# Where the attention's values are summed: two units behind, across sequences, out of one ring of three buffers

## The chip, the core and the metric

One core of a Trainium2 chip runs the whole program. The metric is the device time of one execution in microseconds. The engines are TensorE (PE; its weight loads are listed as PEld), VectorE (DVE), ScalarE (ACT), GpSimd (POOL) and SyncE (SP), whose queue issues most DMAs here. [...]

## The reference

The input is 4 sequences of 1024 tokens with 256 features. Four residual layers follow each other, each behind a layer norm: a linear recurrence with a small MLP, a sparse feed-forward layer (two gated branches that keep the top 32 of 256 features), an attention, and the same feed-forward layer again. The change is in the attention:

```python
q = (x @ Wq.T).reshape(b, t, N_HEADS, HEAD_DIM)
kv_latent = x @ Wkv_down.T
k = (kv_latent @ Wk_up.T).reshape(b, t, N_HEADS, HEAD_DIM)
v = (kv_latent @ Wv_up.T).reshape(b, t, N_HEADS, HEAD_DIM)
scores = jnp.einsum('bqhd,bkhd->bhqk', q, k) * scale
attn = jax.nn.softmax(scores, axis=-1)
out = jnp.einsum('bhqk,bkhd->bqhd', attn, v)
return out.reshape(b, t, N_HEADS * HEAD_DIM) @ Wo.T
```

There are 8 heads of 64 columns, keys and values come from one latent of 64 columns, and the softmax runs over all 1024 tokens.

## The kernel before

The weights are folded, so that the queries meet the latent itself, and the values that are summed are the latent too. Products that need accuracy are made of a high and a low part: `kh` and `kl` for the keys, `la` in f32 or two f16 parts `lb` for the values.

**Units.** `heads` (line 856) goes through one sequence in 32 units. A unit is 128 queries (`q`) of one pair of heads (`g`), and it has two halves (`j`), one head each. There are two blocks of 512 queries (`nb`), so 4 sequences make 128 units and 256 halves. A half does this: four score products into the PSUM tile `sc` (line 886, two buffers), the negated maximum over 1024 keys (line 890, DVE), the exponential with its sum into `ssum` (line 894, ACT) into `pr` (three buffers). Then the probabilities must be transposed, since the product with the values sums over keys.

**Two ways to transpose.** In units with even `q` the probabilities are cast to f16 (line 897, ACT), the remainder is taken on POOL (line 898), and both go through a transposing DMA from SP's queue (line 899) into the tiles `d0` and `d1`, of which there are two each. In units with odd `q` PE transposes in f32 (line 905) into the PSUM tiles `t` (two buffers), and ACT, in the last sequence DVE for one half, copies them (lines 908 and 910) into `p0` and `p1`, of which there is one each.

**The sums.** `values_sum` (line 920) takes the reciprocal of the row sums (DVE), spreads it over 64 columns (line 926, POOL, tile `rows`), multiplies values and transposed probabilities (line 930: 16 products for an f32 unit, 48 for an f16 unit), transposes the reciprocals (line 938), copies them (line 940) and multiplies (line 941) into `on`. Its PSUM bank has the tag `s`, which has two buffers and is shared with all the side work. Two lists hold the units whose sums are due. A unit of the `pending` list (f32) is summed in the first half of the next f16 unit, a unit of the `late` list (f16) in the second half of the next f16 unit. At the end of each sequence what is left in both lists is summed at once (lines 917 and 918). The last group of the last sequence has its units in the order 0, 2, 1, 3.

**Side work.** `merge` (line 963) interleaves the halves of `heads` with the rest by written step numbers: the queries of the next pair, the next sequence's keys and values, the output products (`output`, line 943), the feed-forward tiles of the layer before (24 of 32 tiles run here), and the heads of the next feed-forward layer. That is program order. A planner then decides the final order of each engine's queue from its own estimate of when operands and buffers are free, so a sum may stand several halves behind its place in the program.

## Time and profile before

| | |
|---|---|
| median of 3 runs | 1529.46 us (1526.32 to 1533.48) |
| the profiled execution | 1528.76 us, span 1527.0 us |
| attention stage, first score product to last product of the attention | 376 to 1303 us |
| score products, line 886 | 346.3 us of PE in 1024 matmuls |
| sums, line 930, f32 and f16 | 144.0 and 103.4 us of PE |
| transposes on PE, line 905 | 138.3 us |
| maxima, line 890 | 308.5 us of DVE |
| exponentials, line 894 | 285.9 us of ACT |
| remainders, line 898 | 273.5 us of POOL |
| transposing DMAs, line 899 | 128, 512 KB each read in f16, median 1.92 us on SP's queue |

A line of a group gives the source line, engine, operation, tiles (written <- read), shape and count, then busy time and the mean of one in ns, then the idle time of that engine just before these instructions and which instruction ended it. Busy times of one engine overlap a little where matmuls are pipelined. A wait names the waiting tile and line and the instruction that ended the wait. Granted clock is the share of TensorE's full clock that it was given.

### The profile page before, as it was taken

The page shows a single profiled execution, that of the slowest core. Times are in us where ns is not written, and L with a number is a line of the kernel's source. Part 1 is how long each engine was busy: PE and PEld are TensorE (multiplying, and loading weights), DVE is VectorE, ACT ScalarE, POOL GpSimd, SP SyncE. Part 2 cuts the span into 40 slices and gives each one's busy share as a digit, 9 for nine tenths or more (in the row PEclk, how much of TensorE's full clock was granted, in tenths as well). Part 3 has the DMA queues.
Part 4 walks back from the last instruction along what each step waited for, and adds up shares of the span by engine and source line. Part 5 has one row for each costly group of instructions (what it writes and reads, how often), then busy time and mean ns, then how long its engine had stood idle before and what let it go on. Part 6 is the DMA issues. An engine that isn't in the chain of part 4 may idle for free. (4 is left out here: it accounts for less than half of the span.)

```text
span 1527.0 us, 28727 instructions
## 1 busy us (share of the span) xinstructions
PE 1286.5 (84%) x10134; PEld 955.6 (63%) x10136; DVE 1184.6 (78%) x3682; ACT 1017.5 (67%) x2152; POOL 680.3 (45%) x849
## 2 busy tenths in 40 slices
PE   4879998697898898888998989889999999566675
PEld 3535465376677766766776767677777777334454
DVE  8976665697868887878768687777676675599998
ACT  5353433566887877797777787877777776475674
POOL 2033332161545454544544554454344444067776
PEclk9999999698999999999999999999999999688899
DMA  3110000321454343434433445334344545000000
GB/s 118 32 41 15 21 21 21 128 97 49 84 93 90 61 77 73 77 70 82 82 74 60 72 79 86 61 61 83 68 82 79 92 86 96 1 15 24 22 25 28
DMA packets 288609, 96.51 MB, mean 63 GB/s; under 512 B 268233, under 2 KB 284626, under 8 KB 288466
## 3 DMA queue, kind: packets, MB, share of 16 engines
q1 hardware_dynamic: 283024, 88.50, 28.7%
q10 hardware_dynamic: 5442, 6.18, 1.2%
q8 instruction: 80, 1.31, 0.4%
q14 instruction: 63, 0.52, 0.1%
HBM read 16.01 MB, written 11.53 MB: 18 GB/s over the span
## 5 line engine op out<-in xcount | busy, mean ns | idle before, releaser
L898 POOL TENSOR_TENSOR pd<-pr,pd 128x1024 f16<-128x1024 f32 x128 | 273.5, 2141 | 247.6 <-ACT pd L897 185.7
L890 DVE TENSOR_REDUCE nm<-sc 128x1 f32<-128x1024 f32 x256 | 308.5, 1217 | 78.9 <-PE sc L886 77.5
L894 ACT ACTIVATE pr<-sc,nm 128x1024 f32<-128x1024 f32 x256 | 285.9, 1119 | 84.6 <-DVE nm L892 47.0
L886 PE MATMUL sc<-kh,qs 128*128 128x512 f32 x512 | 184.3, 438 | 26.4 <-ACT pr L894 18.8
L886 PE MATMUL sc<-kl,qs 128*128 128x512 f32 x512 | 162.0, 397 | 0.0
L674 DVE MATCH_REPLACE8 wk<-m,wk 128x256 f32<-128x256 f32 x384 | 154.9, 406 | 0.1
L910 ACT COPY p<-ptp 128x512 f32<-128x512 f32 x224 | 124.1, 590 | 45.3 <-PE ptp L905 33.7
L674 DVE MAX8 m<-wk 128x8 f32<-128x256 f32 x384 | 151.3, 412 | 0.4
L930 PE MATMUL pmo<-p,la 128*64 128x128 f32 x2048 | 144.0, 289 | 6.1 <-ACT ft L524 2.9
L905 PE MATMUL ptp<-ident,pr 128*128 128x128 f32 x1024 | 138.3, 275 | 12.9 <-ACT pr L894 12.4
L930 PEld LDWEIGHTS pmo<-p,la 128*64 128x64 f32 x2048 | 122.8, 144 | 25.0 <-ACT ft L524 5.1
L905 PEld LDWEIGHTS ptp<-ident,pr 128*128 128x128 f32 x1024 | 115.6, 140 | 34.8 <-ACT pr L894 22.2
L897 ACT CAST pd<-pr 128x1024 f16<-128x1024 f32 x128 | 133.5, 1054 | 5.6 <-DMA d<-pd 4.6
L886 PEld LDWEIGHTS sc<-kh,qs 128*128 128x128 f32 x512 | 85.2, 195 | 51.1 <-ACT pr L894 29.8
L886 PEld LDWEIGHTS sc<-kl,qs 128*128 128x128 f32 x512 | 97.0, 190 | 23.2 <-issue 1.4
L930 PE MATMUL pmo<-d,lb 128*64 128x128 f16 x3072 | 103.4, 222 | 7.6 <-DVE qs L853 2.6
L930 PEld LDWEIGHTS <-lb 128*64 128x64 f16 x3072 | 92.2, 111 | 26.3 <-issue 20.1
L628 POOL TENSOR_TENSOR ex<-ex,wk 128x512 f32<-128x512 f32 x61 | 77.6, 1273 | 57.4 <-DVE wk L674 45.5
L926 POOL COPY rows<-rs 128x128 f32<-128x128 f32 x128 | 36.1, 294 | 124.4 <-PE pmo L938 76.3
L941 DVE TENSOR_TENSOR on<-pmo,rb 128x128 f32<-128x128 f32 x128 | 36.4, 285 | 66.8 <-ACT rb L940 66.3
L147 PE MATMUL pt<-ident,xn 128*128 128x128 f32 x256 | 47.8, 309 | 44.5 <-ACT xn L145 32.9
L699 PE MATMUL pf<-wf,vt 128*128 128x256 f32 x288 | 81.2, 427 | 4.6 <-ACT vt L697 4.2
(307 smaller groups left out, 2768.6 us busy)
## 6 DMA issues: line engine op xcount, KB each, us to landing
tt<-ft SPq DMA_DIRECT2D x16, 256.0 KB
tt<-tt SPq DMA_DIRECT2D x8, 512.0 KB
out<-x SPq DMA_DIRECT2D x32, 128.0 KB
x<-in_x ACTq DMA_DIRECT2D x6, 512.0 KB
pf<-pfs SPq DMA_DIRECT2D x12, 256.0 KB
full<-pf SPq DMA_DIRECT2D x24, 128.0 KB
d<-pd SPq DMA_TRANSPOSE x128
wa<-in_w_attn SPq DMA_DIRECT2D x2, 640.0 KB
```

The costliest lines, as they stand in the source:

```text
L147: nc.tensor.transpose(pt[:, k, i * P : (i + 1) * P], xn[:, k * P : (k + 1) * P], ident)
L628: pool.tensor_tensor(ex, ex, wk, ALU.subtract)
L674: ins = make(*args).ins
L699: nc.tensor.matmul(dst, vt[:, k, :], w.wf[:, k, :], start=(k == 0 and bias is None), stop=(k == KD - 1))
L886: nc.tensor.matmul(sc[:, sl], qs[:, j, q * P : (q + 1) * P], kk[:, sl], start=(i == 0), stop=(i == 1))
L890: nc.vector.tensor_reduce(nm, sc, AX.X, ALU.max, negate=True)
L894: nc.scalar.activation(pr, sc, AF.Exp, bias=nm, accum_out=ssum[:, j : j + 1])
L897: nc.scalar.copy(pd[:, 0, :], pr)
L898: nc.gpsimd.tensor_tensor(pd[:, 1, :], pr, pd[:, 0, :], ALU.subtract)
L905: nc.tensor.transpose(pt[:, kk, :], pr[:, kc * P : (kc + 1) * P], self.ident)
L910: nc.scalar.copy(dst, pt)
L930: nc.tensor.matmul(po[j * HD : (j + 1) * HD, 0, :], v, pts[j][:, c, :], start=(n == 0), stop=(n == len(terms) - 1),)
```

## The change

Both lists become one, `due`, which lives in the attention object and so across sequences. Every unit takes one unit out of it: with more than one unit due, the oldest unit's reciprocals are issued in the first half (the new method `reciprocals`) and its sum in the second half. A unit is thus summed in the second half of the second next unit, whatever its kind. Nothing is summed at the end of a sequence, except for the last one, where two units are left. The tiles `d0`, `d1` go; f16 units use `p0` and `p1` too, seen as f16 with twice the columns, and these have three buffers each. `ssum` has six buffers instead of four.

```diff
-        late, pending = [], []
...
-            ssum = sp.tile([P, 2], F32, tag="ssum", name="ssum", bufs=4)
+            ssum = sp.tile([P, 2], F32, tag="ssum", name="ssum", bufs=6)
+            pts = [wp.tile([P, TPB, P], F32, tag=f"p{j}", name=f"p{j}", bufs=3) for j in range(2)]
             if by_dma:
-                pts = [wp.tile([P, 2 * TPB, P], F16, tag=f"d{j}", name=f"d{j}", bufs=2) for j in range(2)]
+                pts = [t.bitcast(F16).rearrange("p c (i q) -> p (c i) q", i=2) for t in pts]
...
             else:
-                pts = [wp.tile([P, TPB, P], F32, tag=f"p{j}", name=f"p{j}") for j in range(2)]
...
-                if j == 0 and pending:
-                    self.values_sum(*pending.pop(0), psum)
-                if j == 1 and late and by_dma != (q > 0 and (b, nb, g) == (B - 1, 1, PAIRS - 1)):
-                    self.values_sum(*late.pop(0), psum)
+                if j == 0 and len(self.due) > 1:
+                    rows = self.reciprocals(self.due[0][2])
+                if j == 1 and len(self.due) > 1:
+                    self.values_sum(*self.due.pop(0), rows, psum)
                 yield
-            (late if by_dma else pending).append((pts, terms, ssum, self.on[b, nb, q][:, g, :]))
-        for args in late + pending:
-            self.values_sum(*args, psum)
+            self.due.append((pts, terms, ssum, self.on[b, nb, q][:, g, :]))
+        if b == B - 1:
+            for unit in self.due:
+                self.values_sum(*unit, self.reciprocals(unit[2]), psum)
...
-    def values_sum(self, pts, terms, ssum, on, psum):
+    def reciprocals(self, ssum):
 
         nc, sp = self.nc, self.sp
         rs = sp.tile([P, 2], F32, tag="rs", name="rs")
         nc.vector.reciprocal(rs, ssum)
         rows = sp.tile([P, 2, HD], F32, tag="rows", name="rows")
         nc.gpsimd.tensor_copy(rows, rs[:, :, None].to_broadcast([P, 2, HD]))
+        return rows
+
+    def values_sum(self, pts, terms, ssum, on, rows, psum):
```

More of the change, by code (lines that the diff above doesn't have):

```diff
@@ L777, in __init__ @@
         self.hp = None
+        self.due = []
         self.k, self.xnt, self.qs, self.on = {}, {}, {}, {}
@@ L926, in values_sum @@
         nc.gpsimd.tensor_copy(rows, rs[:, :, None].to_broadcast([P, 2, HD]))
+        return rows
+    def values_sum(self, pts, terms, ssum, on, rows, psum):
+        nc, sp = self.nc, self.sp
         po = psum.tile([P, 2, P], "s", "pmo")
```

## The prediction

> **What bounds the kernel now.** I read the page first, then the busy time stage by stage, then TensorE's (PE's) own waits in the stage that the diff touches, then who holds a buffer.

> ```profile
> span 1527.0 us, 28727 instructions
> ...
> PE 1286.5 (84%) x10134; PEld 955.6 (63%) x10136; DVE 1184.6 (78%) x3682; ACT 1017.5 (67%) x2152; POOL 680.3 (45%) x849
> ...
> PEclk9999999698999999999999999999999999688899
> ```

> The reader is to see that no engine is saturated over the whole span, and that the clock dips only before and after the middle part. By stage (cut where the score products of line 886 begin and the attention's last product ends, with cuts between at the sequences):

> ```profile
> core 0: us, PE busy (x) PEld busy (x) DVE busy (x) ACT busy (x) POOL busy (x), PEclk, DMA share, GB/s
> 376.00:606.00 230.00, 205.04 (x1996) 160.96 (x1997) 182.25 (x475) 180.43 (x363) 113.28 (x118) 0.99 0.44 80
> 606.00:853.00 247.00, 218.79 (x2143) 173.94 (x2142) 188.62 (x497) 187.78 (x374) 115.47 (x119) 0.97 0.39 74
> 853.00:1096.00 243.00, 215.76 (x2139) 172.06 (x2137) 182.19 (x471) 185.84 (x367) 111.13 (x111) 0.97 0.40 73
> 1096.00:1303.00 207.00, 193.80 (x2125) 157.63 (x2123) 138.93 (x283) 151.60 (x273) 90.17 (x77) 1.00 0.45 83
> 1303.00:1527.00 224.00, 146.23 (x539) 94.94 (x538) 204.02 (x865) 133.64 (x408) 135.95 (x216) 0.84 0.06 20
> ```

> The change lives in the first four rows, 927 us. There PE is busy 205.0 + 218.8 + 215.8 + 193.8 = 833.4 us, so it idles 93.6 us. This stage is paced by PE with small stalls, and 93.6 us is all that any reordering can win. The last row is VectorE's (DVE's) top-k, which the change doesn't touch. What PE's stalls in the stage are:

> ```profile
> PE sc L886 <- ACT pr L894: 18.8, 22, 2.8
> PE ptp L905 <- ACT pr L894: 12.4, 16, 1.8
> PE pt L147 <- DVE qs L853: 9.0, 5, 2.1
> PE sc L886 <- DVE qs L853: 6.7, 7, 1.7
> ...
> L930 PE MATMUL pmo<-p,la 128*64 128x128 f32 x2048 | 144.0, 289 | 6.1 <-ACT ft L524 2.9 <-DVE qs L853 1.8 <-ACT p L910 0.7
> L905 PE MATMUL ptp<-ident,pr 128*128 128x128 f32 x1024 | 138.3, 275 | 12.9 <-ACT pr L894 12.4 <-ACT p L910 0.5
> L930 PE MATMUL pmo<-d,lb 128*64 128x128 f16 x3072 | 103.4, 222 | 7.6 <-DVE qs L853 2.6 <-DMA d<-pd 1.9 <-ACT ex L615 1.9
> ```

> (columns of the first four: total, times, longest.) PE mostly waits for an exponential, to free a score bank or to have something to transpose. The sums of line 930 hardly ever wait for their own data: 0.7 us for a copy by ScalarE (ACT), 1.9 us for a DMA. And the buffers of transposed data, from the lists of line 910 and of SyncE's (SP's) waits:

> ```profile
>   PE ptp L905: 33.7, 32
>   PE pmo L930: 9.0, 4
> ```

> ```profile
> SPq L899 <- POOL pd L898: 238.8, 44, 11.4
> SPq L899 <- PE pmo L930: 194.8, 40, 14.6
> ```

> ACT waited 9.0 us in four places, and SP 194.8 us, until an old sum gave its buffer back. Both rings are already short; SP's wait costs nothing as long as the sum stands far enough back in PE's queue.

> **The change part by part.** A unit is 128 queries of two heads; a half is one head of it. Costs per item from steady stretches of the timeline: four score products 1.6 us, eight transposes 1.1 us, an f32 sum 2.0 us, an f16 sum 1.5 us, its transposed reciprocals 0.33 us.

> *Work.* No product, exponential, copy or DMA comes or goes: 64 f32 and 64 f16 sums, 128 reciprocals, 128 DMA transposes in both. The SBUF is the same: 2x2 and 2x1 tiles of 4 KB a partition before, 2x3 now. So 833 us of PE work stays; only the 93.6 us move.

> *No flush between sequences.* At 856.12 and 857.83 us the two flushed sums of a sequence start without idle time in front of them; their 3.8 us of work is only moved. The gaps around the three boundaries (821 to 860, 577 to 609, 1069 to 1085 us: 6.0, 5.3 and 3.2 us of PE idle) end on exponentials, layer norms and the query split, which all stay. Between 0 and -14.5 us; near the row of the sums themselves, which is 0: I take **-2 us**.

> *Reciprocals half a unit earlier.* PE's transposes of them (line 938) have no idle time before them now, so PE gains 0. On GpSimd (POOL) the copy of 0.29 us waits 76.3 us in all for line 938 two sums earlier, and the subtractions of line 898, whose result the DMA takes, stand behind it for 24.1 us. Their cover is the distance to the f16 sum, below. **0 us.**

> *Sums later.* In the compiled queue of PE I counted how many halves' scores are issued between a unit's own and its sum: f16 units 7.2 before and 7.3 after, f32 units 3.8 and 6.7. The f32 sum had waited 0.7 us for its copy, so that is all there is to win: **0 us**. The transposes of the f32 units also move back, from 1.6 to 2.3 halves after their scores; with 1.22 us (maximum), 1.12 us (exponential), 0.2 us (its accumulator) and some 0.35 us of handing over, a transpose needs 2.9 us of other PE work in front. Before, 13 of 128 have less, short by 8.0 us together; after, 9, short by 3.3 us: **-4.7 us**. The same 2.9 us between scores and the next scores in the same bank: five places, 1.2 us short before, seven, 3.4 us after: **+2.2 us**.

> *One ring of three.* This is the part that can hurt. An f32 unit's copies waited for the sum two units back, and now for the one three back, which is an f16 sum and itself stands 7 halves late; a DMA waited for the sum four units back, now for three. For the DMA: between the old sum's end and the unit's own sum lie at least 12.5 us of PE work before (median 29.5), and 10.8 us after (median 22.5). Two DMA transposes take 2 x 1.9 us to issue on SP, and the last one's data about 2.7 us more in the packets, 6.5 us. So the DMA stays hidden, with 4 us to spare in the worst place; **0 us**, and behind SP's longer waits stand only the loads of line 599, whose data are used after the 16 top-k steps of their tile. For the f32 units: the copy must be made before the second half's transposes find a bank, 1.5 us after the old sum. Before, one place is short by 0.4 us; after, five are, by 7.1 us: **+7 us**. And ACT is in order: behind a copy that waits for its buffer stand the next exponentials, for which PE's scores wait. By the queues, the old sum stands behind the unit's own transposes in 22 of 69 copies before (131 us of PE work in all) and in 36 of 66 after (275 us). With the 9.0 us that ACT really waited before, 9.0 x 275/131 = 18.9, so **+10 us**. Ends: 0, if ACT gets there later than the sum each time; 14 more waits of 9.0/4 = 2.25 us, 31 us.

> [...] PE's waits now are at most 2.8 us long and the stage holds a granted clock of 0.97 to 1.00. [...] I take the row [...].

> *End of the stage.* Two units are left over for the end instead of one, but in both queues the f32 sums of the last two units stand behind the last scores (before: at 1295.7 and 1300.7 us), so 0 to 2 us; **0**.

> Sum: -2 - 4.7 + 2.2 + 7 + 10 = **+12.5 us**. On the profiled execution's own 1528.76 us (span 1527.0 and 1.8 us around it) that is 1541.3; the median is 0.7 us above it, so **1542 us**.

> **The rivals.** *Hidden anyway:* PE has 833 us of work in order, and ACT is at 76% and DVE at 75% of the stage; a late copy is made up before PE runs dry. For it: 194.8 us of SP waits cost PE 1.9 us. Against: ACT, unlike SP, carries the exponentials. 1530 +- 7.6 us. That the planner undoes the change belongs here too, but the compiled queue shows units 30 and 31 summed behind the scores of units 34 and 35, so it doesn't. *Faster:* one mechanism, that the later transposes are always preceded by a finished exponential. Of the 12.4 us of waits at line 905 two thirds go (8 us), and the boundaries give half of their 14.5 us, since nothing there is forced any more: -15, so 1514 us. It decides if ACT's waits for old sums stay under about 10 us in all. [...]

> **How the numbers follow.** Ring waits 0.40 (1534 to 1552), with the clock falling 0.08 (1552 to 1575), hidden 0.22 (1522 to 1537), faster 0.30 (1500 to 1522). Half a per cent, 7.6 us, is what a measurement can tell here. Faster 0.30, same 0.22, slower 0.48. Leaving out a tenth at each end, a third of the faster case and most of the clock case with the top of the ring case, gives 1509 to 1562; the likeliest case alone has 1534 to 1552.

> **What would show it.** In the new profile: waits of the p copies for line 930 of 15 to 25 us instead of 9.0; waits of scores for the exponential above 18.8; transposes' waits below 12.4; f16 sums waiting for the DMA still under 5 us; PE busy in the stage again near 833 us, clock 0.97 or more; the last 224 us unchanged. I am wrong if the p copies wait less than 10 us, or if the f16 sums wait for their DMA by tens of us, or if PE's busy time itself moves.

## The result

The changed kernel takes 1553.76 us (median of 6 runs, 1547.94 to 1561.64) against 1527.45 us for the kernel before (6 runs, 1524.52 to 1533.48) on the same chips: a ratio of 1.0165, 95% interval 1.0137 to 1.0193, so some 25 us slower. I had forecast 1542 us and slower. The direction was right; the size was half of what came, and, as the experiments show, the reason was wrong.

The page of the changed kernel and its busy time by stage, cut at the same places (columns as in the prediction):

```profile
span 1552.7 us, 28808 instructions
...
PE 1301.2 (84%) x10136; PEld 958.8 (62%) x10136; DVE 1183.9 (76%) x3682; ACT 1021.2 (66%) x2152; POOL 681.8 (44%) x849
```

```profile
376.00:607.00 231.00, 203.63 (x1890) 158.45 (x1889) 181.66 (x471) 176.66 (x354) 111.67 (x114) 0.94 0.41 75
607.00:860.00 253.00, 217.87 (x2129) 170.40 (x2129) 188.35 (x496) 188.84 (x374) 114.38 (x116) 0.97 0.41 71
860.00:1110.00 250.00, 216.94 (x2146) 170.24 (x2143) 178.86 (x469) 185.68 (x365) 109.67 (x111) 0.97 0.40 72
1110.00:1330.00 220.00, 206.23 (x2244) 167.78 (x2242) 142.41 (x290) 158.34 (x286) 94.70 (x81) 0.98 0.48 83
1330.00:1553.00 223.00, 147.46 (x540) 95.96 (x538) 204.04 (x865) 133.19 (x408) 136.97 (x216) 0.81 0.06 20
```

The reader is to see that everything happened in the attention stage. It grew from 927 to 954 us by these cuts; the last stage has 223 us, where it had 224. Inside the stage DVE, ACT and POOL do the same work as before. PE is busy for 844.7 us instead of 833.4 (+11.3) and idle for 954 - 844.7 = 109.3 us instead of 93.6 (+15.7).

PE's busy time grew with the same products in it, and the granted clock says why. From here on the stage is taken from its first score product to its last sum exactly (926.9 and 952.5 us), and PE counts as busy where a matmul or a weight load runs: 834.2 us before, 844.7 after. In the records of the clock, 37.5 us of the stage run at half rate before and 62.2 us after; PE is busy in 36.5 and 57.3 us of them. In the changed kernel the starts of two successive transposes (line 905) lie 109 ns apart at full clock and 213 ns at half (medians of 845 and 27 pairs), so I take half of these busy times, 18.2 and 28.6 us, for what the half rate took. Without it 816.0 us remain in both: the same work. So the loss has two parts in this pair of profiles, 15 us of waiting (92.6 to 107.8) and 10 us of half clock.

PE's waits in the stage, and after them those of ACT's copies of transposed data (line 910), of ACT, and of SP, all in the changed kernel:

```profile
PE sc L886 <- ACT pr L894: 36.7, 34, 3.8
PE ptp L905 <- ACT pr L894: 12.1, 14, 2.5
PE ptp L905 <- ACT p L910: 8.9, 14, 1.5
PE pmo L936 <- ACT ft L524: 8.1, 5, 2.6
```

```profile
  PE ptp L905: 26.0, 29
  PE pmo L936: 12.0, 11
```

```profile
ACT pr L894 <- DVE nm L892: 42.3, 35, 2.9
ACT pd L897 <- DMA p<-pd: 38.7, 26, 3.6
```

```profile
SPq L899 <- PE pmo L936: 364.5, 47, 19.2
```

Scores wait for exponentials 36.7 us instead of 18.8. ACT's casts wait 38.7 us for a DMA to let go of their tile, where before it was 4.6 us:

```profile
ACT pd L897 <- DMA d<-pd: 4.6, 3, 2.2
```

SP waits 364.5 us for old sums instead of 194.8. That looks like a short ring: a DMA waits for its slot, keeps its cast tile, and the exponential behind the next cast on ACT is held up. In one of these waits ACT stood idle for 3.41 us until the cast started at 945.97 us; the maximum for the exponential behind it was ready at 944.34 us, and that started at 946.93. The copies' own wait for old sums, my dearest item, rose only from 9.0 to 12.0 us.

### The profile page after: what moved, and what is told of

It is laid out like the page before. It is cut to its first block, busy times and chain, and to the rows that moved or that the text cites. A ratio compares the mean times of both kernels' runs of the same rounds, so it can differ in the third digit from the quotient of the medians.

```text
span 1552.7 us, 28808 instructions
## 1 busy us (share of the span) xinstructions
PE 1301.2 (84%) x10136; PEld 958.8 (62%) x10136; DVE 1183.9 (76%) x3682; ACT 1021.2 (66%) x2152; POOL 681.8 (44%) x849
## 4 chain that ended last, share of the span: by engine, by line
PE 35%; DVE 33%; ACT 12%; DMA 8%; issue 6%; POOL 4%; ACTq 0%; SPq 0%; POOLq 0%; DVEq 0%
DVE wk L674 8%; PE pmo L936 7%; DMA p<-pd 7%; PE sc L886 6%; DVE m L674 6%; DVE nm L890 6%; ACT pr L894 4%; PE ptp L905 3%; PE po L437 3%; PE pu L170 2%; ACT pd L897 2%; PE pmy L170 2%; DVE qs L854 1%; PE pz L452 1%; POOL pd L898 1%
## 5 line engine op out<-in xcount | busy, mean ns | idle before, releaser
L898 POOL TENSOR_TENSOR pd<-pr,pd 128x1024 f16<-128x1024 f32 x128 | 274.0, 2144 | 205.0 <-ACT pd L897 151.1
L894 ACT ACTIVATE pr<-sc,nm 128x1024 f32<-128x1024 f32 x256 | 286.2, 1121 | 77.8 <-DVE nm L892 42.3
L886 PE MATMUL sc<-kh,qs 128*128 128x512 f32 x512 | 185.0, 440 | 42.1 <-ACT pr L894 36.7
L886 PE MATMUL sc<-kl,qs 128*128 128x512 f32 x512 | 164.6, 402 | 0.0
L905 PE MATMUL ptp<-ident,pr 128*128 128x128 f32 x1024 | 143.9, 280 | 21.4 <-ACT pr L894 12.1
L897 ACT CAST pd<-pr 128x1024 f16<-128x1024 f32 x128 | 134.3, 1054 | 39.3 <-DMA p<-pd 38.7
L674 DVE MATCH_REPLACE8 wk<-m,wk 128x256 f32<-128x256 f32 x384 | 159.0, 421 | 0.1
L674 DVE MAX8 m<-wk 128x8 f32<-128x256 f32 x384 | 155.4, 426 | 0.3
L910 ACT COPY p<-ptp 128x512 f32<-128x512 f32 x224 | 124.5, 591 | 38.8 <-PE ptp L905 26.0
L905 PEld LDWEIGHTS ptp<-ident,pr 128*128 128x128 f32 x1024 | 118.0, 143 | 46.1 <-ACT pr L894 18.3
L936 PE MATMUL pmo<-p,la 128*64 128x128 f32 x2048 | 135.8, 282 | 7.3 <-DVE on L947 4.4
L936 PEld LDWEIGHTS pmo<-p,la 128*64 128x64 f32 x2048 | 116.5, 140 | 25.6 <-issue 11.3
L886 PEld LDWEIGHTS sc<-kh,qs 128*128 128x128 f32 x512 | 86.2, 197 | 71.4 <-ACT pr L894 54.6
L936 PE MATMUL pmo<-p,lb 128*64 128x128 f16 x3072 | 105.0, 225 | 13.4 <-ACT ft L524 8.1
L886 PEld LDWEIGHTS sc<-kl,qs 128*128 128x128 f32 x512 | 97.8, 192 | 21.9
L947 DVE TENSOR_TENSOR on<-pmo,rb 128x128 f32<-128x128 f32 x128 | 36.7, 286 | 82.3 <-ACT rb L946 81.7
L556 PE MATMUL pl<-lint,xc_f 128*128 128x512 f32 x128 | 73.5, 662 | 9.6 <-ACT xc_f L587 9.6
```

The source lines that it names most:

```text
L556: self.last_logits = nc.tensor.matmul(v, x, w.lint, start=False, stop=True).ins
L674: ins = make(*args).ins
L886: nc.tensor.matmul(sc[:, sl], qs[:, j, q * P : (q + 1) * P], kk[:, sl], start=(i == 0), stop=(i == 1))
L894: nc.scalar.activation(pr, sc, AF.Exp, bias=nm, accum_out=ssum[:, j : j + 1])
L897: nc.scalar.copy(pd[:, 0, :], pr)
L898: nc.gpsimd.tensor_tensor(pd[:, 1, :], pr, pd[:, 0, :], ALU.subtract)
```

## The experiments

Ratios are to the kernel before, run on the same chip.

**The flush and the ring, one at a time.** Only the flush is removed:

```diff
-        late, pending = [], []
+        late, pending = self.late, self.pending
...
-        for args in late + pending:
-            self.values_sum(*args, psum)
+        if b == B - 1:
+            for args in late + pending:
+                self.values_sum(*args, psum)
```

> The kernel before, with the two lists kept across sequences and emptied at the very end only; tiles and order of sums as before. If holding the data too long in the shared ring costs the time (theory A), this has no part in it: within 0.5% of before, 1520 to 1535 us. If it is the missing flush, which lets the last sums of a sequence fall between the next sequence's scores (theory B), a good part of the 26 us shows: 1540 us or more. If any new order of the queues costs some 1% (theory C), 1535 to 1550.

Measured 1531.87 us, 1.0013 (0.9998 to 1.0029). The flush is not the cause, and its removal brings nothing either.

Only the ring, with order of sums and flush as before:

```diff
+            pts = [wp.tile([P, TPB, P], F32, tag=f"p{j}", name=f"p{j}", bufs=3) for j in range(2)]
             if by_dma:
-                pts = [wp.tile([P, 2 * TPB, P], F16, tag=f"d{j}", name=f"d{j}", bufs=2) for j in range(2)]
+                pts = [t.bitcast(F16).rearrange("p c (i q) -> p (c i) q", i=2) for t in pts]
...
-                pts = [wp.tile([P, TPB, P], F32, tag=f"p{j}", name=f"p{j}") for j in range(2)]
```

> The kernel before, its order of sums and its flush, but with the one ring of three for both kinds of transposed data. A DMA then waits for an f32 sum, which this order makes early, and f32 copies wait for an f16 sum. Theory A (a DMA that waits for its slot keeps its cast tile, and the next cast on ScalarE waits for that): casts wait under 10 us in all, SyncE waits for old sums less than 195 us, time 1520 to 1535. If the ring itself is at fault in whatever order (theory B2): casts wait 30 us or more, 1545 to 1560.

Measured 1529.87 us, 1.0000 (0.9988 to 1.0012). Its waits are those of before:

```profile
PE sc L886 <- ACT pr L894: 18.6, 21, 2.7
PE ptp L905 <- ACT pr L894: 11.5, 14, 1.8
```

Both edits together (and six `ssum` buffers), which is the whole change except for when f32 units are summed and when reciprocals are issued:

> The ring of three and no flush, but f32 units still summed in the first half of the next f16 unit: the whole change except that sums of f32 units come later and reciprocals earlier. Theory A: the late f32 sum is what holds the slot that a DMA waits for, so 1520 to 1538 us and casts wait under 10 us. If ring and missing flush together are the cause: 1545 to 1560.

Measured 1529.91 us, 0.9997 (0.9978 to 1.0016). The ring of three costs nothing in this order. What is left of the change is the later sums, with what they do to the ring, and the reciprocals.

**The later sums with the tiles of before** (two for f16, one for f32 data):

> The changed kernel's order of sums, with the tiles of before: two for f16 data, one for f32 data. A DMA waits for the sum four units back again, and so ScalarE's casts wait for DMAs under 10 us; but an f32 unit's copies must wait for the sum two units back, which now comes late. Theory A says that the DMA's side is healed; the f32 side gets worse, copies of transposed data wait for sums by 40 us or more, and transposes pile up: 1545 to 1590. If the order of sums alone were at fault and not the buffers, it would stay at 1550 to 1558.

Measured 1553.52 us, 1.0146 (1.0129 to 1.0163). In its profile (an execution 11 us longer than the median) ACT's copies wait three times as long for old sums as in the changed kernel:

```profile
ACT p L910 <- PE pmo L936: 35.6, 21, 3.3
```

ACT's casts wait 0.2 us for DMAs, where the changed kernel has 38.7, and the time is about the same. A ring that is shared is not needed for the loss.

**More buffers.** These need SBUF, so I gave the feed-forward side tiles one buffer instead of two, and ran that alone as a base.

```diff
-        fp = c2.enter_context(tc.tile_pool(name="f_s", bufs=2))
+        fp = c2.enter_context(tc.tile_pool(name="f_s", bufs=1))
```

> The changed kernel with one buffer instead of two for each tile of the feed-forward side work during the attention: it frees 7 KB a partition, so that more buffers fit in the next three runs, and is their base. The side work is spread thinly, so all theories expect 1550 to 1565 us, with ScalarE's casts still waiting some 39 us for DMAs.

Measured 1555.56 us, 1.0168 (1.0140 to 1.0196), as the changed kernel: a fair base in this order of sums.

> The base with three instead of two tiles of cast probabilities. Theory A (a DMA late for its slot keeps its cast tile, so ScalarE's next cast and all exponentials behind it wait): the casts' 39 us of waits shrink below 10 us, and 10 to 25 us of the time come back. If the DMA's lateness has no part in it (theory D: only the copies of f32 units that wait for old sums, as I predicted): no change, within 4 us of the base.

With `pd` at `bufs=3`: 1556.29 us, 1.0176 (1.0153 to 1.0198). The casts' waits fall from the base's 40.6 us to less than half, and nothing comes back:

```profile
ACT pd L897 <- DMA p<-pd: 18.0, 11, 3.8
```

> The base with a ring of four instead of three. Theories A and D both expect the loss to go, since both DMAs and copies get their slot a unit earlier: 1520 to 1535 us, SyncE's waits for old sums far below 364 us. If only the order of the sums costs (theory C), no change from the base.

With `p0`, `p1` at `bufs=4`: 1557.47 us, 1.0172 (1.0141 to 1.0203). Again the waits go where they should, and the time doesn't follow:

```profile
SPq L899 <- PE pmo L936: 195.1, 35, 16.9
...
ACT pd L897 <- DMA p<-pd: 15.7, 9, 4.7
```

SP is back at 195 us, the value of the kernel before. So the most visible new waits of the changed kernel, SP's and the casts', are not what costs the time.

> The base with four instead of three tiles of probabilities. If f32 units whose transposes wait for a slot starve the exponentials of a place to write (theory E), 10 us or more come back; theory A expects no more than 5 us, since the cast tiles stay held.

With `pr` at `bufs=4`: 1554.36 us, 1.0154 (1.0130 to 1.0179). A further buffer brings no time back for any of the three SBUF tiles. Theories A, D and E fall. The PSUM tiles `sc`, `t` and `s` kept their two buffers in every run, and stay untested.

**The reciprocals.** DVE's groups show a wait that has grown (first line before, second after):

```profile
L924 DVE RECIPROCAL rs<-ssum 128x2 f32<-128x2 f32 x128 | 15.4, 153 | 21.2 <-ACT pr L894 20.6 <-issue 0.2 <-POOL rows L926 0.2
L925 DVE RECIPROCAL rs<-ssum 128x2 f32<-128x2 f32 x128 | 20.1, 157 | 64.0 <-ACT pr L894 53.8 <-POOL rows L927 10.0
```

In the trace 68 of these 128 reciprocals start within 1 us of the end of their own unit's second exponential: the planner takes them far ahead, and DVE then stands with the next maxima behind them. That doesn't come from issuing them half a unit earlier: if the reciprocals are issued together with the sum again, the compiled program has the same queue on every engine. I put it down to the sums being in unit order, which puts an f16 unit's reciprocal ahead of the next f32 unit's. The first run holds the reciprocals of the changed kernel back, behind the newest maximum on DVE (`latest`); the second (its edit is not shown) issues them at the end of their own unit in the order of e3:

```diff
-                    rows = self.reciprocals(self.due[0][2])
+                    with self.tc.issue_after(latest):
+                        rows = self.reciprocals(self.due[0][2])
```

> The changed kernel, with each reciprocal tied behind the newest maximum in VectorE's queue, so that it stands 3 maxima behind its unit's own instead of 0 to 1 (by the compiled queue 2.97 on average against 1.02 for f16 and 0.77 for f32 units). Sums and transposes stand where they stood. Theory F (the reciprocal, pulled ahead by the planner, waits at the head of VectorE's queue for its own unit's exponential, and holds up the maxima and so the exponentials and scores): VectorE's idle time before reciprocals falls from 64 us to under 10, and 15 us or more come back, 1525 to 1540. Theory G (the place of the f32 sums alone: late, and in the unit that also has the transposes, so that PE's load is uneven): 1548 to 1558, no change.

Measured 1571.06 us, 1.0282 (1.0266 to 1.0298). The wait is gone, and the kernel is a further 1.2% slower, which neither theory expected:

```profile
L926 DVE RECIPROCAL rs<-ssum 128x2 f32<-128x2 f32 x128 | 19.6, 154 | 0.1
```

```profile
DVE on L948 <- ACT rb L947: 112.3, 53, 6.1
```

The second view says why the run is no clean test: the last step of each sum, which needs the reciprocals, now waits longer too (112.3 us, against 81.7 in the changed kernel and 66.3 before).

> Ring of three without flush and f32 sums early as before (the run that stayed at the time of before), but every reciprocal issued at the end of its own unit: by the compiled queue the f16 units' reciprocals stand 0.75 maxima behind their own instead of 2.44. Theory F: VectorE waits some 50 us or more before reciprocals, and the time goes to 1540 to 1555. Theory G: no change, 1525 to 1537.

Measured 1536.53 us, 1.0055 (1.0038 to 1.0072). The same wait is put into the fast order:

```profile
L927 DVE RECIPROCAL rs<-ssum 128x2 f32<-128x2 f32 x128 | 20.3, 159 | 64.5 <-ACT pr L895 48.5 <-POOL rows L929 15.4
```

It costs 0.55%, some 8 us, and less than theory F asked for. So the reciprocals can explain up to a third of the loss, if their cost adds to the rest. What they cost in the slow order alone stays open.

**Late, or in the wrong unit?** The first kernel makes the f32 sums late, but leaves them in f16 units. It has no flush, a ring of four, six `ssum` buffers and the small side tiles; only the line that moves the sums is shown. The second moves the f16 sums instead, a unit later and into the f32 units, and leaves the f32 sums early; it has the tiles of before, no flush and six `ssum` buffers.

```diff
-                if j == 0 and pending:
+                if j == 0 and len(pending) > 1:
```

> Order of before without flush, but each f32 unit summed in the first half of the second next f16 unit, three units later instead of one, from a ring of four (with the small pool of the feed-forward tiles, whose own effect was 2 us). The f32 sums so come as late as in the changed kernel (7.4 halves behind their own scores in the compiled queue, 6.7 there, 4.0 in the early order), but never in a unit that also has PE's transposes. Theory G1 (late f32 sums cost, wherever they stand): 1545 to 1560. Theory G2 (sum and transposes in the same unit, so that PE's load swings between the two kinds of unit): 1525 to 1537.

Measured 1552.28 us, 1.0169 (1.0145 to 1.0193). It isn't the unit: late f32 sums cost as much as in f3, which has the same tiles, when no transposes stand in the same unit. (The early order with a ring of four and the small side tiles was not run; e3 and f1 show each kind of edit to be free where it was tried.) Its waits are not those of the changed kernel:

```profile
PE sc L887 <- ACT pr L895: 17.2, 14, 3.6
PE ptp L906 <- ACT pr L895: 16.4, 17, 2.1
```

Scores wait for exponentials no longer than in the kernel before (18.8 us), and the loss is there all the same.

```diff
-                if j == 1 and late and by_dma != (q > 0 and (b, nb, g) == (B - 1, 1, PAIRS - 1)):
+                if j == 1 and (len(late) > 1 if not by_dma else len(late) > 2):
```

> Tiles and early f32 sums of before, no flush, but each f16 unit is summed in the second half of the f32 unit three units later instead of the f16 unit two later. PE's own load is then the most even of all: a f16 unit has 2.3 us of sums, a f32 unit 2.2 us of transposes and 1.9 us of sums, against 4.2 and 2.2 before and 1.9 and 4.5 in the changed kernel. Theory G2 in the sense of an even load: 1515 to 1530, no slower than before. If any sum in the unit with the transposes costs: 1540 or more. G1: no change, 1525 to 1535.

Measured 1572.47 us, 1.0297 (1.0269 to 1.0326). The most even load on paper gives the slowest kernel. PE's waits of this run:

```profile
PEld sc L887 <- ACT pr L895: 47.9, 40, 3.6
PE sc L887 <- ACT pr L895: 34.6, 28, 2.9
PEld ptp L906 <- ACT pr L895: 30.4, 24, 4.1
PE ptp L906 <- ACT pr L895: 22.8, 20, 3.6
```

This run changes three things at once: the f16 sums are later, they stand in the units with the transposes, and the two buffers of `d0` and `d1` are given back a unit later (SP waits 381.8 us for old sums, ACT's casts 21.1 us for DMAs). Which of them costs was not taken apart.

**What follows.** Every kernel in which a sum was put later in the program lost 1.4% or more: with f32 sums late the changed kernel, e4, f1 to f4 and g3, in either kind of unit, with one, three or four buffers; h1, where reciprocals were late as well; and g4 with late f16 sums. The kernels with the early sums stayed within 0.2% in their medians, or lost 0.55% to their reciprocals. The traces show that the sums really came later. In the order in which PE ran its matmuls, the scores of 3.6 to 4.0 further halves, on average, run between an f32 unit's own scores and its sum in before, e1, e2, e3 and h2, and those of 6.4 to 7.3 halves in the others except g4. g4 has 4.0 for f32 units; for f16 units it has 8.3, where all the others have 6.9 to 7.7.

By the stage's records, PE idles (neither matmul nor weight load) 90.3 to 92.6 us in before, e1, e2 and e3, 99.4 in h2, and 103.4 to 122.2 in all the others. PE's work at full clock, counted as above, is 810 to 823 us in all of them. So the loss is waiting plus half clock and no added work. It is shown that moving the f32 sums later brings it.

Why is only narrowed, and this much is argued, not shown: the sums are what PE can do while scores and transposes wait for an exponential, and the planner places them differently when they come late. Which of its choices makes the gaps was not settled; no single count of the queues that I made (work between scores of one bank, work between a unit's scores and its transposes, swings over four halves) separates the fast from the slow kernels clearly. One rival is untested. The time that PE idles just before it writes a sum's tile `pmo` does separate them: 7.3 to 11.6 us in the fast kernels and h2, 13.6 to 25.6 in the slow ones. In the changed kernel the largest item of it is the wait of 8.1 us for ACT to copy a side tile `ft` out of the shared banks `s` (2.9 us before). So late sums may collide with the side work for these two banks, or that wait may be another consequence; no run gave `s` a third buffer. No variant beat the kernel before.

## Why the prediction was right, and where it was wrong

- **What bounds the stage:** right. PE paces it, its work stayed, and the change could move some 94 us of idle time. I had not counted that the busy time itself can grow with the clock; it grew by 11.3 us, one of the three signs of being wrong that I had named.
- **No flush, -2 us:** nothing (e1: 1.0013).
- **Reciprocals half a unit earlier, 0 us:** right as put, since the planner makes the same queues of it. But unit order moves the f16 reciprocals ahead of their own exponentials; I looked only at PE's line 938 and POOL's copy and not at what stands behind the reciprocal on DVE. Worth up to 8 us by h2, where I had put 0.
- **Sums later, 0 us, transposes -4.7 us, banks +2.2 us:** this is the step that failed. I argued that a sum which waited 0.7 us for its data can only gain by being late. What I left out is what else PE then has at hand: the waits at the transposes were 12.1 us plus a new 8.9 us for copies, instead of less than 12.4, and the waits of scores for exponentials rose by 17.9 us, not 2.2. The changed kernel against e3, and g3, show that late f32 sums cost some 1.7%. Through which wait stays open: g3 loses as much with scores that wait no longer than before.
- **One ring of three, +17 us:** wrong. The ring costs 0.0% with early sums (e2, e3); with late ones neither the old tiles (e4) nor a fourth buffer (f3) give anything back, and ACT's waits for old sums were 12.0 us, not 18.9. I also gave the DMA's longer wait 0 us since the sum is far behind, and missed that it keeps the cast tile; that wait is real, 38.7 us, but worth nothing by f2 and e4.
- **The clock:** I took the row, "0.97 to 1.00". The row is a mean that hides the drops: 37.5 us at half rate were in the stage already. 62.2 us after, PE being busy in 57.3 of them, cost 10 us more. In windows of 3.41 us, the grid told of below, that is some 18 at half rate instead of 11, and some 1.6 us for each (28.6 us over 18, 18.2 over 11). The range that I gave to a falling clock, 1552 to 1575 us, was my own estimate, worked out from no drop in the trace of before. This part varies between executions: the profiled ones of e1 and e3 have granted clocks of 0.934 and 0.938 over the program, the lowest of their twelve runs each, with 91.6 and 90.3 us of idle time in the stage, and are 4 to 5 us longer than their medians. So the 10 us belong to this pair of profiles; that the clock is lower on the whole shows in the averages over the program, 0.935 in the changed kernel's six runs and 0.943 in 31 of the kernel before.
- **The sum:** +12.5 us forecast, some 25 us measured. The forecast owes its direction to a ring that costs nothing, which is luck; the missing terms are the lateness and the clock. The measured time lies in the range of the case that I gave 0.08, the clock's.

## What to carry to other kernels

In a queue that a planner fills, work that is ready early is not free to come late (here 1.7%), even where it had hardly waited for its own data; so ask of a moved step what the engine has left to do where it used to stand. A new wait that is large in the profile, and even one with a clear story of cause, may cost nothing; add the buffer that would heal it before believing it. And compare idle time and clock apart: busy time minus half of the busy time at half rate told here whether there was more work (816.0 us in both).

## What the runs showed of the hardware

In the attention stage the granted clock fell to half after windows in which PE had still worked. Two such windows and the drops behind them, in the changed kernel (columns as in the table of stages, the granted clock third from the right):

```profile
787.70:791.10 3.40, 1.52 (x18) 1.05 (x20) 3.34 (x12) 3.35 (x7) 2.37 (x2) 1.00 0.00 0
791.20:794.50 3.30, 3.30 (x42) 2.94 (x37) 3.21 (x8) 1.90 (x5) 0.29 (x1) 0.50 0.02 5
930.90:934.40 3.50, 0.94 (x28) 0.81 (x28) 0.89 (x1) 2.63 (x4) 1.14 (x1) 1.00 1.06 210
934.50:937.90 3.40, 3.40 (x34) 2.15 (x29) 0.00 (x0) 3.32 (x7) 3.09 (x3) 0.51 0.01 2
```

PE was busy for 1.52 of 3.40 us and for 0.94 of 3.50, in several pieces (the longest gaps in them are 1.8 and 2.5 us), and the next 3.4 us ran at half rate although PE was busy throughout (3.30 of 3.30 us and 3.40 of 3.40). Over the profiles of before and after, the 22 drops inside the stage follow a stretch of 3.4 us in which PE was busy for 0 to 66%, and in 21 of them no single gap filled it.

| PE busy in the window | windows | followed by a drop |
|---|---|---|
| under 40% | 10 | 10 |
| 40 to 50% | 9 | 7 |
| 50 to 67% | 45 | 5 |
| more | 456 | 0 |

So in these two traces all 10 windows under 40% were followed by a drop, none of the 456 above 67%, and some of those between. The ends of matmuls are modelled in the profile, so a window near the border of two rows can't be placed for certain. In the two windows shown PE idled for 1.88 and 2.56 us, and behind them it worked for 3.30 and 3.40 us at half rate, half of which is lost by the estimate above.
